# Where two sums are made: VectorE, GpSimd and PSUM in a hybrid of convolution, attention and experts

## The chip, the cores and the metric

The kernel runs on one core of a Trainium2 chip, in fp32 throughout. The metric is the device time of one execution in microseconds; the lower the better. The core has a TensorE (PE in the profile, its weight loads PEld), which multiplies matrices into PSUM; VectorE (DVE), ScalarE (ACT) and GpSimd (POOL), which work on elements; and SyncE (SP), which here issues the DMAs. The engines run beside each other, each through its own queue in program order, and wait for one another by semaphores.

## What is computed

The input x is 8 images of 128 channels and 36 x 36 places. Two layers follow, each with a residual sum. Cut to what matters:

```python
# layer 0: after a group norm, 1x1 and 3x3 convolutions give x, q, k, v;
# attention from 1296 places to 1156 places, then a 1x1 convolution and tanh
attn = softmax(einsum('ancq,bncd->anbqd', q, k), axis=-1)
a_x  = einsum('bncd,anbqd->anbcq', v, attn)[0]
h    = tanh(conv(concat([x, a_x, v_c]), w_h) + b_h)
x    = x0 + conv(h, w_o) + b_o

# layer 1: tokens t [8, 1296, 128]; additive attention, then experts chosen per expert
q = einsum('bld,ed->ble', ln(t), Wq) + bq
k = einsum('bld,ed->ble', ln(t), Wk) + bk
scores = einsum('bijd,d->bij', tanh(q[:, :, None, :] + k[:, None, :, :]), w) + bw
t = t + einsum('bij,bjd->bid', softmax(scores), ln(t))
t = t + experts(ln(t))          # gate, top 8 tokens of each of 64 experts, two layers, scatter
```

The second line of `concat` that comes from the constant image c0 is a vector and enters as a bias. The additive attention is by far the largest part: 8 x 1296 x 1296 x 128 values of tanh.

## The kernel before

tanh(q + k) is not computed element by element. Features of q and of k are made as exponentials of signed sums of channels, so that a product of matrices gives, for each group of channels, a numerator and a denominator, and the score is a sum of their quotients. Such a pair of products is a slot. SLOTS (lines 48 to 53) lists the NP = 12 slots of a unit: four blocks give two slots each with 32 rows a half, and four give one with 64 rows a half; the latter are slots 2, 5, 8 and 11.

A unit is (image b, chunk c, key tile j): 432 queries against 128 keys. There are 8 x 3 x 10 full units of 12 slots, and 24 with the remaining 16 keys (three slots), so 240 x 12 + 72 = 2952 slots. The main loop (from line 934 on) walks through the slots. The order of work is written out by hand: each engine's queue is what this loop emits. For a slot p it emits

- the steps of background lanes that are due (`take_turns`),
- `numerators(p)`: two products on TensorE (L793) into two PSUM buffers of the pool ps_n, which has four buffers and is shared with all background products (`aux`),
- `denominators(p + LAG)`, three slots ahead: two products (L793) into a buffer d, Ln of them on ACT (L815), and after every second slot Exp of the negated Ln (L818), which makes reciprocals lq,
- `terms(p)` on VectorE: numerator times lq,
- a background matmul turn if one is due (`matmul_turn`; PACE and `balance` space them: each turn counts its columns, each slot earns 370).

`terms` has two ways. In most slots VectorE multiplies each half from PSUM into a buffer rp in SBUF (L846; the pool rpp has three buffers) and GpSimd adds both halves to accp in one instruction (L851 for slot 1, L853 later; slot 0 has no add of its own). In the slots of DVE_PAIRS (line 58) VectorE multiplies within PSUM (L836, L840) or into accd (L835) and adds both halves to accd itself (L837, L842). At the end of a unit `sums` puts accp's halves and accd together on GpSimd (L860, L863), and seven slots later ACT makes the exponential e of the scores (L878).

The background lanes hold generators that yield between a turn of matmuls and the step that takes its result out of PSUM. Three matter here. `attend` follows a chunk: for each of its four groups of 108 queries, products of e with the normalized tokens xh (and a column of ones, which gives the denominator) go in two turns into pa; the first is copied to sums in SBUF (L625), the second added to it (L628), then come the reciprocal of the last column (L630), the product with it and the residual token t (L631) and the statistics (L635, L636). `layer0` prepares the next image: for each of three chunks it makes the exponentials e of the scores (L381), their running sum tot on GpSimd (L374), then five turns of products pa with the values, summed in ax (L395, L397), then the column sum pt of tot by a product with ones, its reciprocal ri as Exp of a negated Ln on ACT (L405, L406), and ax times ri (L412), added to the 1x1 convolution px (L413). Query features qf for the coming chunk (L593 on ACT, L594 on GpSimd) come during the chunk's last unit. After the last unit the experts run alone (from line 971 on).

Of the kernel before, what the change touches and what calls it, by code (L numbers as in the profile page):

```python
# [10 lines left out]
AF = mybir.ActivationFunctionType  # L11
ALU = mybir.AluOpType
AX = mybir.AxisListType

NB, C, H, W = 8, 128, 36, 36
N = H * W
HV, WV = H - 2, W - 2
D = HV * WV
CH = 432
NCH = N // CH  # L20
RC = H // NCH
T = 108
# [5 lines left out]
DT = 116  # L28
DTILES = [(o, min(DT, D - o)) for o in range(0, D, DT)]
NDT = len(DTILES)  # L30
# [24 lines left out]
IN_TURN = [m + i for m in range(NF // 2) for i in (0, NF // 2)]  # L55
LAG = 3
SHIFT = 6.5
DVE_PAIRS = (2, 5, 8, 11)
PACE = 370

REM_SLOTS = [([q + m for m in range(NF // 2)], rows) for q, rows in SLOTS[:3]]
# [3 lines left out]
def kernel(  # L65
# [28 lines left out]
    nc = tc.nc  # L94
# [26 lines left out]
    with ExitStack() as loop, ExitStack() as score:  # L121
# [25 lines left out]
        def chunk_tile(name):  # L147
            return chunks.tile([128, CH], F32, tag="chunk", name=name)

        def aux(name):  # L150
            return ps_n.tile([128, 512], F32, tag="n", name=name)
# [25 lines left out]
        ones = const.tile([128, 128], F32, tag="ones", name="ones")  # L177
# [47 lines left out]
        TAKE = (False, 1)  # L225

        def step(rest=1):
            return (False, rest)

        def matmuls(rest=0):  # L230
            return (True, rest)
# [3 lines left out]
        def bmm(out, lhsT, rhs, **kw):  # L235
            behind[0] += max(out.free_size(), 128) + 20
            mm(out, lhsT, rhs, **kw)  # L237
# [91 lines left out]
        def layer0(b):  # L329

            r = xs[b][:, :N]
            k = convolved.pop("k")
            while gates:
                yield step()
            wv_t = load_taps(w_v, "wv_t")
            v = big_tile("v0")
            wq_t = load_taps(w_q, "wq_t")
            yield matmuls(3)
            for r0, nr in KROWS:
                yield from conv_turns(  # L340
                    wv_t, (r0, nr), 1, 1, WV, v[:, r0 * WV : (r0 + nr) * WV]
                )
            yield matmuls(1)

            vw = big_tile("vw")[:DT, : NDT * C].rearrange("p (j c) -> p j c", c=C)
            for g in range(0, NDT, 4):
                some = DTILES[g : g + 4]
                tp = aux("pvw")
                for j, (o, n) in enumerate(some):
                    bmm(tp[:n, j * C : (j + 1) * C], v[:, o : o + n], wh_s[:, 1, :],  # L350
                       start=True, stop=True)
                yield TAKE
                full = sum(n == DT for _, n in some)
                nc.vector.tensor_copy(
                    vw[:, g : g + full, :],
                    tp[:DT, : full * C].rearrange("p (j c) -> p j c", c=C),
                )
                for j in range(full, len(some)):
                    n = some[j][1]
                    nc.vector.tensor_copy(vw[:n, g + j, :], tp[:n, j * C : (j + 1) * C])  # L360
                yield matmuls()
            hp = big_tile("hpre")[:, :N]
            for c in range(NCH):
                cols = slice(c * CH, (c + 1) * CH)
                q = chunk_tile("q0")
                yield from conv_turns(wq_t, (c * RC, RC), 0, 0, W, q)
                yield matmuls(1)
                tot = chunk_tile("tot0")
                ex = []

                def total(j):
                    n = DTILES[j][1]
                    of = ex[0] if j == 1 else tot
                    nc.gpsimd.tensor_add(tot[:n], of[:n], ex[j][:n])  # L374

                for o, n in DTILES:
                    ps = aux("s0")
                    bmm(ps[:n, :CH], k[:, o : o + n], q, start=True, stop=True)
                    yield TAKE
                    e = chunk_tile("e0")  # L380
                    nc.scalar.activation(e[:n], ps[:n, :CH], AF.Exp)  # L381
                    ex.append(e)
                    if len(ex) > 2:
                        total(len(ex) - 2)
                    yield matmuls()
                ax = chunk_tile("ax0")
                for j0 in range(0, NDT, 2):
                    pa = aux("pa0")
                    for j in (j0, j0 + 1):
                        n = DTILES[j][1]  # L390
                        bmm(pa[:, :CH], vw[:n, j, :], ex[j][:n], start=(j == j0), stop=(j > j0))
                    yield TAKE
                    if j0 == 0:
                        total(NDT - 1)
                        nc.vector.tensor_scalar(ax, pa[:, :CH], 1.0 / D, None, ALU.mult)  # L395
                    else:
                        nc.vector.scalar_tensor_tensor(  # L397
                            ax, pa[:, :CH], 1.0 / D, ax, ALU.mult, ALU.add
                        )
                    yield matmuls()  # L400
                pt = aux("pt0")
                bmm(pt[:, :CH], ones[:DT], tot[:DT], start=True, stop=True)
                yield TAKE
                ri = chunk_tile("ri0")
                nc.scalar.activation(ri, pt[:, :CH], AF.Ln, scale=1.0 / D)  # L405
                nc.scalar.activation(ri, ri, AF.Exp, scale=-1.0)  # L406
                yield matmuls(1)
                px = aux("px1")
                bmm(px[:, :CH].rearrange("p (a b) -> p a b", b=W), wh_s[:, 0, :],
                   xpad[:, 1 + c * RC : 1 + (c + 1) * RC, 1 : 1 + W], start=True, stop=True)  # L410
                yield TAKE
                nc.vector.tensor_mul(ax, ax, ri)  # L412
                nc.vector.tensor_add(hp[:, cols], px[:, :CH], ax)  # L413
                yield matmuls()
            yield step(2)
            nc.scalar.activation(hp, hp, AF.Tanh, bias=hb)
            nc.scalar.preload_act_table_set(LNEXP)
            yield matmuls(2)
            for c in range(NCH):
                cols = slice(c * CH, (c + 1) * CH)  # L420
                po = aux("po0")
                bmm(po[:, :CH], wo_s, hp[:, cols], start=True, stop=True)
                yield TAKE
                nc.vector.scalar_tensor_tensor(
                    r[:, cols], po[:, :CH], bo_s, r[:, cols], ALU.add, ALU.add
                )
                yield matmuls()
# [173 lines left out]
        def attend(b, c, es):  # L601


            xh, _, xr = prepared[b]
            if c == 0:
                t2 = big_tile("t2").rearrange("p (t c) -> p t c", c=128)
                mv = two.tile([T, NT, 2], F32, tag="t2_mv", name="t2_mv")
                attended[b] = (t2, mv)
            t2, mv = attended[b]
            for i in range(TPC):  # L610
                at = c * TPC + i
                nc.sync.dma_start(t2[:T, at, :], tokd[b][at * T : (at + 1) * T])
                sums = two.tile([T, C + 1], F32, tag="sums", name="sums")
                for some in (range(6), range(6, NKT)):
                    pa = aux("pa1")[:T, : C + 1]
                    for j in some:
                        if j < NKT - 1:
                            e, v = es[j][:, i * T : (i + 1) * T], xh[:, j, :]
                        else:
                            rows = slice(32 * i, 32 * i + REM)  # L620
                            e, v = es[j][rows, :T], xr[rows]
                        bmm(pa, e, v, start=(j == some[0]), stop=(j == some[-1]))
                    yield TAKE
                    if j < NKT - 1:
                        nc.vector.tensor_copy(sums, pa)  # L625
                        yield matmuls()
                    else:
                        nc.vector.tensor_add(sums, pa, sums)  # L628
                inv = small.tile([T, 1], F32, tag="inv", name="inv")
                nc.vector.reciprocal(inv, sums[:, C : C + 1])  # L630
                nc.vector.scalar_tensor_tensor(  # L631
                    t2[:T, at, :], sums[:, :C], inv, t2[:T, at, :], ALU.mult, ALU.add
                )
                st = small.tile([T, 6], F32, tag="t2_st", name="t2_st")
                nc.vector.bn_stats(st, t2[:T, at, :])  # L635
                nc.vector.bn_aggr(mv[:, at, :], st)  # L636
                yield matmuls()
            if c == NCH - 1:
                prepared.pop(b)
            if b == NB - 1:  # L640
                yield from gate_logits(b, [c])
# [292 lines left out]
        for p, (u, k) in enumerate(slots):  # L934
            b, c, j = units[u]
# [213 lines left out]
```

## Time and profile before

Times are microseconds. Three runs of the kernel before and the profiled execution:

| | us |
|---|---|
| median of 3 runs | 6438.8 |
| lowest, highest | 6434.69, 6439.65 |
| the profiled execution, its own time | 6428.4 |
| its span | 6426.7 |

The profile is one execution, with a mean granted TensorE clock of 0.966. A busy time is the time in which an engine executed something; its share is of the span. A group is all instructions of a line, engine and shape; "idle before" is the time that the engine stood still just ahead of them, with what ended it. Rows of the slots and of the two background parts:

| line, engine, what | count | busy us | mean ns |
|---|---|---|---|
| L846 DVE, product into rp (128 x 432) | 3984 | 2202.6 | 600 |
| L840 DVE, product within PSUM (128 x 432) | 1440 | 811.7 | 608 |
| L842 DVE, sum into accd (128 x 432) | 1440 | 867.4 | 602 |
| L853 POOL, both halves into accp (128 x 864) | 1464 | 2965.2 | 2025 |
| L860, L863 POOL, end of a unit (128 x 432) | 264, 240 | 290.8, 265.6 | 1101, 1107 |
| L815 ACT, Ln of both halves | 2952 | 2552.6 | 882 |
| L818 ACT, Exp over two slots (128 x 1728) | 1464 | 2406.8 | 1644 |
| L628, L630, L631 DVE, attend | 96 each | 28.0, 15.7, 87.9 | 292, 164, 915 |
| L397, L412 DVE, attention of layer 0 | 96, 24 | 58.3, 19.6 | 607, 816 |

Between a short head (about 200 us, before the first slots) and a tail (about 200 us, the experts) the busy shares are even: the slots of one image run beside the preparation of the next and the gating of the last.

### The profile page before, as it was taken

The numbers are of one execution on the slowest core, as the hardware profiler recorded it, in microseconds if no ns is written. First come the engines' busy times: TensorE is split into PE (matmuls) and PEld (weight loads), VectorE is DVE, ScalarE is ACT, GpSimd is POOL, SyncE is SP. The second block draws the span as 40 slices with busy tenths as digits, with TensorE's granted clock in tenths as the row PEclk, the third lists the DMA queues.
The fourth block names the chain that finished last, engine by engine and source line by source line (L and its number), as shares of the span: only waits on it lengthen the run. The fifth ranks groups of instructions, "written<-read, shape, count | busy, mean of one in ns | idle before, by whom it ended". The sixth has DMA issues, their size and how long they took to land.

```text
span 6426.7 us, 106771 instructions
## 1 busy us (share of the span) xinstructions
PE 6054.8 (94%) x40448; PEld 2813.9 (44%) x40448; DVE 4900.4 (76%) x9315; ACT 5354.6 (83%) x5426; POOL 4798.1 (75%) x2966
## 2 busy tenths in 40 slices
PE   8999999999999999999999999999999999999986
PEld 4444444444444444444444444444444444544432
DVE  3687778877788777888788887887778877778862
ACT  1788898888888888888888888888888888989970
POOL 3677777787777877777787787778777787888870
PEclk9999999999999999999999999999999999999997
DMA  0200011000110002100111001100011000100017
GB/s 28 66 31 23 22 63 36 30 24 27 56 46 19 24 27 68 33 26 22 44 47 38 22 23 53 43 32 25 20 63 43 23 24 27 61 26 28 24 66 253
DMA packets 155284, 265.78 MB, mean 41 GB/s; under 512 B 53712, under 2 KB 79824, under 8 KB 154768
## 3 DMA queue, kind: packets, MB, share of 16 engines
q1 hardware_dynamic: 154768, 258.95, 12.5%
q8 instruction: 318, 5.21, 0.3%
q14 instruction: 198, 1.62, 0.1%
HBM read 196.81 MB, written 61.83 MB: 40 GB/s over the span
## 4 chain that ended last, share of the span: by engine, by line
PE 67%; DVE 12%; ACT 7%; issue 7%; POOL 6%; DMA 1%; SPq 0%; POOLq 0%; DVEq 0%; ACTq 0%
PE n L793 30%; PE d L793 10%; PE pc L237 7%; PE pa L237 6%; ACT lq L815 5%; DVE n L840 3%; DVE rp L846 3%; PE s L237 3%; PE pk L237 3%; PE pq L237 2%; DVE accd L842 2%; POOL accp L853 2%; DVE t L631 1%; PE n L800 1%; POOL t L681 1%
## 5 line engine op out<-in xcount | busy, mean ns | idle before, releaser
L853 POOL TENSOR_TENSOR accp<-accp,rp 128x864 f32<-128x864 f32 x1464 | 2965.2, 2025 | 1028.0 <-DVE rp L846 975.3
L793 PE MATMUL n<-qf,kf 32*128 32x432 f32 (+1 forms) x11520 | 3239.2, 579 | 93.4 <-DVE rp L846 47.0
L815 ACT ACTIVATE lq<-d 128x864 f32<-128x864 f32 x2952 | 2552.6, 882 | 690.7 <-PE d L793 643.3
L793 PE MATMUL d<-qf,kf 32*128 32x432 f32 (+1 forms) x11520 | 2876.6, 568 | 21.2 <-ACT lq L815 16.4
L846 DVE TENSOR_TENSOR rp<-n,lq 128x432 f32<-128x432 f32 x3984 | 2202.6, 600 | 623.7 <-PE d L793 399.3
L818 ACT ACTIVATE lq<-lq 128x1728 f32<-128x1728 f32 x1488 | 2429.0, 1632 | 47.1
L793 PEld LDWEIGHTS n<-qf,kf 32*128 32x128 f32 (+1 forms) x11520 | 1167.1, 187 | 1703.4 <-DVE rp L846 586.3
L793 PEld LDWEIGHTS d<-qf,kf 32*128 32x128 f32 (+1 forms) x11520 | 1038.8, 188 | 392.2 <-issue 254.1
L840 DVE TENSOR_TENSOR n<-n,lq 128x432 f32<-128x432 f32 x1440 | 811.7, 608 | 280.1 <-PE n L793 239.2
L842 DVE TENSOR_TENSOR accd<-n,accd 128x432 f32<-128x432 f32 x1440 | 867.4, 602 | 24.7
L851 POOL TENSOR_TENSOR accp<-rp 128x864 f32<-128x864 f32 x264 | 533.8, 2022 | 221.1 <-DVE rp L846 217.5
L237 PE MATMUL pa<-xh,e 128*108 128x129 f32 x1920 | 262.6, 284 | 55.6 <-DVE rp L846 34.7
L860 POOL TENSOR_TENSOR accp<-accp 128x432 f32<-128x432 f32 x264 | 290.8, 1101 | 16.2
L237 PEld LDWEIGHTS pa<-xh,e 128*108 128x108 f32 x1920 | 223.3, 175 | 179.1 <-DVE rp L846 107.4
L594 POOL TENSOR_SCALAR qf<-qf,cs_s 128x432 f32<-128x432 f32 x192 | 262.7, 1374 | 42.0 <-ACT qf L593 42.0
L863 POOL TENSOR_TENSOR accd<-accp,accd 128x432 f32<-128x432 f32 x240 | 265.6, 1107 | 28.5 <-DVE accd L842 10.4
L237 PE MATMUL s<-q,k 128*116 128x432 f32 x480 | 229.8, 570 | 3.3 <-DVE q L260 2.1
L237 PEld LDWEIGHTS pk<-xT,a_k 128*128 128x128 f32 x1408 | 172.2, 193 | 109.8 <-DVE accd L842 27.6
L374 POOL TENSOR_TENSOR tot<-tot,e 116x432 f32<-116x432 f32 x192 | 212.0, 1104 | 6.1
L835 DVE TENSOR_TENSOR accd<-n,lq 128x432 f32<-128x432 f32 x240 | 144.9, 604 | 91.6 <-PE n L793 60.5
L381 ACT ACTIVATE e<-s 116x432 f32<-116x432 f32 x240 | 125.0, 521 | 106.6 <-PE s L237 105.5
L237 PE MATMUL pk<-xT,a_k 128*128 128x128 f32 (+1 forms) x1408 | 203.2, 288 | 2.6 <-DVE accd L842 2.3
(175 smaller groups left out, 4144.4 us busy)
## 6 DMA issues: line engine op xcount, KB each, us to landing
kf<-kd SPq DMA_DIRECT2D x240, 512.0 KB
kd<-ks SPq DMA_DIRECT2D x160, 256.0 KB
w<-in_weight_dram SPq DMA_DIRECT2D x32, 1024.0 KB
x<-in_x_dram SPq DMA_DIRECT2D x8, 648.0 KB
t<-tokd SPq DMA_DIRECT2D x96, 54.0 KB
t2d<-t2T SPq DMA_DIRECT2D x24, 216.0 KB
res<-t2d SPq DMA_DIRECT2D x8, 648.0 KB
out_dram<-res SPq DMA_DIRECT2D x8, 648.0 KB
```

The costliest lines, as they stand in the source:

```text
L237: mm(out, lhsT, rhs, **kw)
L594: nc.gpsimd.tensor_scalar(qf[:, 1, :], qf[:, 0, :], cs_s[:, q : q + 1], None, ALU.mult)
L793: mm(outs[h][:, :CH], kf[rows[h], q, :], qf_of[b, c, q][rows[h], part, :], start=True, stop=True)
L815: nc.scalar.activation(lq[:, o : o + 2, :], d[:, :, :CH], AF.Ln)
L818: nc.scalar.activation(some, some, AF.Exp, scale=-1.0)
L840: mult(ns[h], ns[h], lq[:, o + h, :])
L842: nc.vector.tensor_add(live["d"], ns[h], live["d"])
L846: mult(rp[:, h, :], ns[h], lq[:, o + h, :])
L851: nc.gpsimd.tensor_add(live["p"], live["r"], rp)
L853: nc.gpsimd.tensor_add(live["p"], live["p"], rp)
L860: nc.gpsimd.tensor_add(s[:, 0, :], s[:, 0, :], s[:, 1, :])
L863: nc.gpsimd.tensor_add(d, s[:, 0, :], d)
```

## The change

DVE_PAIRS loses slot 11, so that its products go into rp and its sum to GpSimd, ahead of `sums`. In `attend` the second sum is written over pa in PSUM instead of sums in SBUF, and the reciprocal and the product read it there. In `layer0` the first partial product is copied without the factor 1/D, and Ln of pt loses it too; the middle ones are plain sums; pt with its Ln and Exp comes ahead of the last of the five turns; the last sum is written over pa in PSUM, and the product with ri reads it from there, ahead of the turn of px.

```diff
-DVE_PAIRS = (2, 5, 8, 11)
+DVE_PAIRS = (2, 5, 8)
@@ layer0
                 ax = chunk_tile("ax0")
+                ri = chunk_tile("ri0")
                 for j0 in range(0, NDT, 2):
-                    pa = aux("pa0")
+                    if j0 == NDT - 2:
+                        pt = aux("pt0")
+                        bmm(pt[:, :CH], ones[:DT], tot[:DT], start=True, stop=True)
+                        yield TAKE
+                        nc.scalar.activation(ri, pt[:, :CH], AF.Ln)
+                        nc.scalar.activation(ri, ri, AF.Exp, scale=-1.0)
+                        yield matmuls()
+                    pa = aux("pa0")[:, :CH]
                     for j in (j0, j0 + 1):
                         n = DTILES[j][1]
-                        bmm(pa[:, :CH], vw[:n, j, :], ex[j][:n], start=(j == j0), stop=(j > j0))
+                        bmm(pa, vw[:n, j, :], ex[j][:n], start=(j == j0), stop=(j > j0))
                     yield TAKE
                     if j0 == 0:
                         total(NDT - 1)
-                        nc.vector.tensor_scalar(ax, pa[:, :CH], 1.0 / D, None, ALU.mult)
+                        nc.vector.tensor_copy(ax, pa)
+                    elif j0 < NDT - 2:
+                        nc.vector.tensor_add(ax, pa, ax)
                     else:
-                        nc.vector.scalar_tensor_tensor(
-                            ax, pa[:, :CH], 1.0 / D, ax, ALU.mult, ALU.add
-                        )
+                        nc.vector.tensor_add(pa, pa, ax)
+                        nc.vector.tensor_mul(ax, pa, ri)
                     yield matmuls()
-                pt = aux("pt0")
-                bmm(pt[:, :CH], ones[:DT], tot[:DT], start=True, stop=True)
-                yield TAKE
-                ri = chunk_tile("ri0")
-                nc.scalar.activation(ri, pt[:, :CH], AF.Ln, scale=1.0 / D)
-                nc.scalar.activation(ri, ri, AF.Exp, scale=-1.0)
-                yield matmuls(1)
                 px = aux("px1")
...
                 yield TAKE
-                nc.vector.tensor_mul(ax, ax, ri)
                 nc.vector.tensor_add(hp[:, cols], px[:, :CH], ax)
@@ attend
                     if j < NKT - 1:
                         nc.vector.tensor_copy(sums, pa)
                         yield matmuls()
-                    else:
-                        nc.vector.tensor_add(sums, pa, sums)
+                nc.vector.tensor_add(pa, pa, sums)
                 inv = small.tile([T, 1], F32, tag="inv", name="inv")
-                nc.vector.reciprocal(inv, sums[:, C : C + 1])
+                nc.vector.reciprocal(inv, pa[:, C : C + 1])
                 nc.vector.scalar_tensor_tensor(
-                    t2[:T, at, :], sums[:, :C], inv, t2[:T, at, :], ALU.mult, ALU.add
+                    t2[:T, at, :], pa[:, :C], inv, t2[:T, at, :], ALU.mult, ALU.add
                 )
```

## The prediction

> **What bounds the kernel now.** I read the page first (shares of the engines, the chain), then the chain summed by line, then the waits, then single lines and one stretch of the timeline, last a table of stretches for the engine that gets the work. The page:
>
> ```profile
> span 6426.7 us, 106771 instructions
> PE 6054.8 (94%) x40448; PEld 2813.9 (44%) x40448; DVE 4900.4 (76%) x9315; ACT 5354.6 (83%) x5426; POOL 4798.1 (75%) x2966
> PE 67%; DVE 12%; ACT 7%; issue 7%; POOL 6%; DMA 1%; SPq 0%; POOLq 0%; DVEq 0%; ACTq 0%
> ```
>
> Four engines are busy between 75% and 94%, and no single one is full: the chain that ended last is two thirds TensorE, 12% VectorE and 6% GpSimd. The DVE part is where the change can save, the POOL part where it can lose. The chain by line shows which DVE instructions those are:
>
> ```profile
> by line: PE n L793 30.4%; PE d L793 9.6%; PE pc L237 7.2%; issue 6.9%; PE pa L237 6.4%; ACT lq L815 4.9%; DVE n L840 3.3%; DVE rp L846 3.0%; PE s L237 3.0%; PE pk L237 2.7%; PE pq L237 2.1%; DVE accd L842 1.7%; POOL accp L853 1.6%; DVE t L6
> ```
>
> L840 and L842 are the products and sums of slots 5, 8 and 11, whose sums VectorE makes. They have 5.0% of the chain with 3 x 240 slots; L846, the products of all other slots, has 3.0% with 1992 (3984 instructions, two a slot). The reason is in the waits (who waited for whom, us in total, times, longest):
>
> ```profile
> PEld n L793 <- DVE accd L842: 248.3, 535, 3.3
> DVE rp L846 <- POOL accp L851: 78.1, 32, 8.7
> DVE rp L846 <- POOL accp L853: 3.1, 5, 1.1
> ```
>
> The numerators of a later slot need the PSUM buffers of an earlier one, and where VectorE sums, it holds them for four instructions instead of two. The other two lines are the reverse: VectorE wants an rp buffer that GpSimd has not added up yet. That is rare today, 37 times and 81 us of 6427.
>
> One more DVE line stands out, the product of attend (durations min/median/max), and the timeline beside it says why:
>
> ```profile
> L631 DVE SCALAR_TENSOR_TENSOR t<-sums,inv,t x96: 350/674/1841, 456.6 to 6274.5; 108x128 f32<-108x128 f32 x96
> ...
> 3018.48 2.02 POOL L853 TENSOR_TENSOR accp<-accp,rp 128x864 f32<-128x864 f32 x1 [0.75 <-DVE rp L846]
> ...
> 3019.03 1.61 DVE L631 SCALAR_TENSOR_TENSOR t<-sums,inv,t 108x128 f32<-108x128 f32 x1
> ```
>
> A 0.35 us instruction took 1.61: it began 0.55 us into a GpSimd add and ended at 3020.64, just after that add's end at 3020.50.
>
> **What the Trainium skill says.** "SBUF — State Buffer", section "Who interferes with whom": a VectorE instruction with two SBUF inputs contends with a GpSimd instruction that reads SBUF, and the one that comes second blocks until the first is done; with at most one SBUF input, outside the two-port modes, it does not. The trace agrees twice: L631 reads sums and t, both in SBUF, and spreads from 350 to 1841 ns; L846 reads PSUM and SBUF and stays within 542 to 611 ns over 3984 instructions beside a GpSimd that is 75% busy. "PSUM — Partial Sum Buffer", section "Specifications (TRN2)": VectorE reads and writes PSUM, at most one tensor input from there. The new forms keep to that, and writing into PSUM costs nothing here: L840 (PSUM to PSUM) has a mean of 608 ns, L846 (PSUM to SBUF) 600. The engine prices come from rows: 602 ns for an L842 add, 2025 ns for an L853 add over both halves.
>
> **The change part by part.** The sum is made against the profiled execution's own 6428.4 us (span 6426.7, 1.7 around it); the median of the runs is 10.4 higher, and I add that at the end.
>
> A. Slot 11 leaves VectorE: 240 x 2 L842 adds go, 289 us of DVE work (480 x 0.602). Its products become L846 products and its PSUM buffers come free after two instructions. What that is on the path, from the chain: 5.0% of 6426.7 is 321 us for three slot kinds, so 107 for slot 11; as an ordinary slot it still has L846's share, 193 us / 1992 x 240 = 23. Saved: 84 us. Bounds: nothing, if TensorE's own queue or ACT (83% busy) is late next everywhere; 289 us if every add stood on the path, which a 12% DVE share excludes as a likely value. I take 84.
>
> B. The same slot reaches POOL: 240 more L853 adds of 2.025 us, 486 us, so POOL goes from 75% to 82% of an unchanged span. Its idle time today is 1629 us, so on average the work fits. It does not everywhere. Five of the ten full units of one chunk, us of the stretch and then the busy us (and instructions) of PE, PEld, DVE, ACT and POOL, the granted clock and the DMA columns:
>
> ```profile
> 1280.30:1303.90 23.60, 23.39 (x117) 9.58 (x116) 19.28 (x36) 21.04 (x22) 16.82 (x11) 1.00 0.08 22
> 1303.90:1331.40 27.50, 27.11 (x356) 11.87 (x358) 18.57 (x33) 24.19 (x28) 26.46 (x19) 1.00 0.08 23
> ...
> 1384.90:1410.40 25.50, 25.11 (x122) 9.83 (x126) 18.43 (x34) 23.35 (x28) 24.91 (x18) 1.00 0.07 25
> 1410.40:1432.80 22.40, 22.02 (x113) 8.91 (x106) 18.75 (x34) 21.05 (x22) 16.77 (x10) 1.00 0.08 21
> 1432.80:1458.50 25.70, 24.76 (x113) 9.64 (x116) 19.58 (x35) 23.67 (x28) 23.78 (x16) 1.00 0.05 12
> ```
>
> A plain unit has some 6 us to spare; the three of the ten that also carry the attention's running total (L374) or the query products (L594) have 1.0, 0.6 and 1.9 and get 2.0 more: 2.5 us over per chunk, 60 us over 24 chunks if nothing took it up. Much is taken up by the plain unit behind it; what isn't appears as VectorE waiting for an rp buffer. In the queue, slot 11's add stands just ahead of the two adds of sums (1.1 us each), which stand ahead of L851 of the next unit; so L851, the one waited for today, ends up to 2.0 us later. The 37 waits of today grow by 2.0 (75 us), and I estimate that as many more that just miss today grow by half of that (37): 112 us of DVE idle. VectorE's waits reach the end only where TensorE has no other work, so half: +55. Bounds 0 and +146 (three loaded units a chunk, 2.025 us each, 24 chunks). What else waits behind POOL is TensorE's transposes of t and xh (L681, L538); this is inside the bound.
>
> C. Attend. L628's sum goes to PSUM, still one instruction (294 ns, taken unchanged), the reciprocal reads one PSUM column (164), and the product now has one SBUF tensor: 915 mean becomes about 350, its minimum, 96 times: 54 us. L631 takes 1.5% to 1.7% of the chain in the stretches of 1000 us from 1200, 2200 and 4200 us, 15 to 17 us, and is busy about as much there (96 x 0.915 = 88 us over six such stretches), so nearly all of it is on the path; TensorE's next numerators are late next, so I take 80%: -43. Against it, the pa buffer is held through reciprocal and product, about 0.6 us longer; in a pool of four the numerators two slots on can want it. Nobody waits for L628 in the trace. Bounds 0 and 96 x 0.6 = 58, taken +10. In the queue behind the product stand the two statistics and the terms of the slot, which move up.
>
> D. Attention of layer 0: the final product changes from ax, ri (two SBUF inputs, 816 mean, 1329 at most) to pa, ri; 24 x 0.21 = 5 us saved. The ax chain has seven DVE instructions before and after at about 607 each; 1/D goes from both sides and removes no instruction. The sum of the exponentials (pt) comes one turn earlier and its Ln and Exp (512 and 563 ns) have one turn less before the DVE add and product need ri. ACT's queue ahead of them holds at most a pair's Exp, so a stall of 0.2 to 0.5 us behind which the slot's terms queue: 24 x 0.2 = 5. Net 0, bounds -5 and +25. The running total has still three turns of pa before pt, so POOL is not late for it.
>
> Sum: -84 + 55 - 43 + 10 = -62; 6428.4 - 62 = 6366, and with the 10.4 the predicted median is 6377 us, 1.0% faster.
>
> **The rivals.** R1, slower: POOL becomes the bound at the ends of loaded units. A lag above some 4.5 us (three slots of about 2.17 us between a product and the reuse of its rp buffer, less the add's 2.0) stops VectorE, and with it the release of PSUM and TensorE. For it: three units in ten go over their length, and the L851 waits already reach 8.7 us. Against it: the six spare microseconds of the plain units. Price: +146 from B, +10 from C, A down to 60 because those units don't gain, C's 43: +53, or about 6492. R2, VectorE was the tighter bound: half of the 289 us is gained (-145), the plain units take up most of POOL's work (+15), C gives its whole 54 and no buffer is late: -184, 6255. For it: the DVE is 68% to 84% busy in the stretches above and stands between TensorE's numerators and their buffers; against it, ACT's 83%. R3, A and B cancel: what VectorE doesn't wait for in PSUM it waits for in rp. Then C alone stays, -33, 6406.
>
> **How the numbers follow.** Forecast 0.37 (its own range 6340 to 6395), R2 and what lies between 0.16, R3 0.22, R1 0.25. A measurement here tells 0.2% (13 us) from no change. Faster by more: the forecast, R2 and half or more of R3, 0.64; within: the upper end of R3 and the lower of R1, 0.10; slower 0.26. The range 6270 to 6485 leaves out the extremes of R2 and R1.
>
> **What would show it.** A right: L842 has 960 instructions, and the waits of PEld n for accd fall by a third or more from 248 us. B right: L853 x1704, POOL at 82 to 84%, and the waits of DVE rp for POOL between 130 and 250 us; over 350 is R1. C right: L631's median near 350 with a maximum under 450; wrong if it still spreads. D right: no DVE wait for ri above 10 us. The whole is wrong if POOL's share of the chain rises by more than DVE's falls.

## The result, and the profile after

The changed kernel takes 6512.6 us (median of 4 runs, 6503.9 to 6528.4) where the kernel before takes 6436.7: a ratio of 1.0123, with a 95% interval from 1.0100 to 1.0145. It is 1.2% slower, 79 us by the ratio (76 between the two medians); the forecast was 1% faster, and the time lies above the range that it gave.

The page of the changed kernel: span, busy shares, chain by engine.

```profile
span 6526.6 us, 107021 instructions
PE 6181.5 (95%) x40448; PEld 2868.2 (44%) x40448; DVE 4595.9 (70%) x8835; ACT 5368.6 (82%) x5426; POOL 5270.3 (81%) x3206
PE 66%; POOL 11%; DVE 8%; issue 7%; ACT 6%; DMA 1%; SPq 0%; POOLq 0%; ACTq 0%; DVEq 0%
```

VectorE lost 304 us of busy time (4900 to 4596) and GpSimd gained 472, about as counted. The chain shows what that did: DVE went from 12% to 8%, POOL from 6% to 11%. The forecast had named a POOL share that rises by more than DVE's falls as the sign that it would be wrong as a whole.

The waits of the changed kernel (who waited for whom, us in total, times, longest):

```profile
PEld n L793 <- DVE accd L842: 204.3, 393, 3.4
DVE rp L846 <- POOL accp L851: 163.5, 91, 5.5
DVE rp L846 <- POOL accp L853: 112.8, 79, 4.0
```

VectorE's waits for an rp buffer rose from 81 us (37 times) to 276 (170 times). The waits on accd fell only from 248 to 204.

The product of attend is now L631 with pa as its input (durations min/median/max), and here the forecast, a median near 350 ns and a maximum under 450, holds:

```profile
L631 DVE SCALAR_TENSOR_TENSOR t<-pa,inv,t x96: 349/351/353, 461.7 to 6372.6; 108x128 f32<-108x128 f32 x96
```

Where is the time? The unit of image 4, chunk 2, key tile 6 is the costliest place. In the windows view (stretch, its length, busy us of PE, PEld, DVE, ACT and POOL, granted clock, DMA columns) it took this before:

```profile
3918.30:3943.90 25.60, 22.29 (x121) 10.75 (x119) 18.82 (x36) 20.29 (x20) 25.20 (x23) 0.85 0.07 25
```

and this after:

```profile
3970.90:4004.10 33.20, 26.65 (x136) 12.37 (x135) 18.00 (x33) 22.93 (x23) 27.93 (x20) 0.90 0.12 36
```

Its timeline after, GpSimd and VectorE alone:

```profile
3975.11 2.01 POOL L853 TENSOR_TENSOR accp<-accp,rp 128x864 f32<-128x864 f32 x1
3977.11 1.56 POOL L539 TENSOR_SCALAR xh<-tok,ln_mv,ln_rs 128x128 f32<-128x128 f32 x2
3978.65 2.01 POOL L853 TENSOR_TENSOR accp<-accp,rp 128x864 f32<-128x864 f32 x1
3980.73 1.10 POOL L860 TENSOR_TENSOR accp<-accp 128x432 f32<-128x432 f32 x1
3981.91 1.10 POOL L863 TENSOR_TENSOR accd<-accp,accd 128x432 f32<-128x432 f32 x1
3983.00 2.33 POOL L539 TENSOR_SCALAR xh<-tok,ln_mv,ln_rs 128x128 f32<-128x128 f32 x3
3985.31 1.99 POOL L851 TENSOR_TENSOR accp<-rp 128x864 f32<-128x864 f32 x1
...
3980.69 1.12 DVE L846 TENSOR_TENSOR rp<-n,lq 128x432 f32<-128x432 f32 x2 [0.73 <-POOL accp L853]
3981.73 0.68 DVE L557 COPY xT<-tpc 128x512 f32<-128x512 f32 x1
3987.33 1.12 DVE L846 TENSOR_TENSOR rp<-n,lq 128x432 f32<-128x432 f32 x2 [4.92 <-POOL accp L851]
```

From 3975.11 on GpSimd has no gap of 0.1 us for over 12 us: adds of the slots, the normalized tokens xh of the next image, the end of the unit (L860, L863), and only then the add of slots 0 and 1 (L851) that sets an rp buffer free. VectorE stands still for 4.92 us until 3987.33, and numerators and Ln wait behind it too. In the images 1 to 6 the unit of chunk 2, key tile 6 is 5 to 11 us longer than before.

### The profile page after: what moved, and what is told of

It reads as the page before. It is cut to its first block, busy times and chain, and to the rows that moved or that the text cites. A ratio compares the mean times of both kernels' runs of the same rounds, so it can differ in the third digit from the quotient of the medians.

```text
span 6526.6 us, 107021 instructions
## 1 busy us (share of the span) xinstructions
PE 6181.5 (95%) x40448; PEld 2868.2 (44%) x40448; DVE 4595.9 (70%) x8835; ACT 5368.6 (82%) x5426; POOL 5270.3 (81%) x3206
## 4 chain that ended last, share of the span: by engine, by line
PE 66%; POOL 11%; DVE 8%; issue 7%; ACT 6%; DMA 1%; SPq 0%; POOLq 0%; ACTq 0%; DVEq 0%
PE n L793 29%; PE d L793 10%; PE pc L237 7%; PE pa L237 7%; POOL accp L853 5%; ACT lq L815 4%; DVE rp L846 3%; PE s L237 3%; PE pk L237 2%; DVE n L840 2%; POOL accp L851 2%; PE pq L237 2%; PE d L800 1%; DVE accd L842 1%; POOL qf L595 1%
## 5 line engine op out<-in xcount | busy, mean ns | idle before, releaser
L853 POOL TENSOR_TENSOR accp<-accp,rp 128x864 f32<-128x864 f32 x1704 | 3447.7, 2023 | 889.7 <-DVE rp L846 823.4
L793 PE MATMUL n<-qf,kf 32*128 32x432 f32 (+1 forms) x11520 | 3332.3, 586 | 122.6 <-DVE rp L846 83.9
L846 DVE TENSOR_TENSOR rp<-n,lq 128x432 f32<-128x432 f32 x4464 | 2464.4, 600 | 1112.0 <-PE d L793 488.2
L793 PE MATMUL d<-qf,kf 32*128 32x432 f32 (+1 forms) x11520 | 2997.3, 573 | 46.1 <-ACT lq L815 42.3
L793 PEld LDWEIGHTS n<-qf,kf 32*128 32x128 f32 (+1 forms) x11520 | 1203.2, 189 | 1788.5 <-DVE rp L846 712.5
L793 PEld LDWEIGHTS d<-qf,kf 32*128 32x128 f32 (+1 forms) x11520 | 1078.4, 190 | 428.0 <-issue 245.2
L840 DVE TENSOR_TENSOR n<-n,lq 128x432 f32<-128x432 f32 x960 | 543.9, 609 | 191.3 <-PE n L793 136.2
L842 DVE TENSOR_TENSOR accd<-n,accd 128x432 f32<-128x432 f32 x960 | 577.8, 602 | 16.4
L851 POOL TENSOR_TENSOR accp<-rp 128x864 f32<-128x864 f32 x264 | 533.9, 2022 | 14.4 <-DVE rp L846 14.3
L860 POOL TENSOR_TENSOR accp<-accp 128x432 f32<-128x432 f32 x264 | 291.1, 1102 | 20.4
L237 PE MATMUL pa<-xh,e 128*108 128x129 f32 x1920 | 268.3, 287 | 37.2 <-DVE t L631 16.5
L863 POOL TENSOR_TENSOR accd<-accp,accd 128x432 f32<-128x432 f32 x240 | 265.1, 1105 | 18.8
L237 PE MATMUL pa<-e,vw 116*128 116x432 f32 x480 | 203.1, 549 | 1.6 <-DVE rp L846 0.6
```

The costliest lines, as they stand in the source:

```text
L793: mm(outs[h][:, :CH], kf[rows[h], q, :], qf_of[b, c, q][rows[h], part, :], start=True, stop=True)
L840: mult(ns[h], ns[h], lq[:, o + h, :])
L842: nc.vector.tensor_add(live["d"], ns[h], live["d"])
L846: mult(rp[:, h, :], ns[h], lq[:, o + h, :])
L851: nc.gpsimd.tensor_add(live["p"], live["r"], rp)
L853: nc.gpsimd.tensor_add(live["p"], live["p"], rp)
```

## The experiments

All ratios are of a run against the kernel before on the same chip, with 95% intervals. Unless a diff says otherwise it is against the kernel before.

**psum_only**: the changed kernel with DVE_PAIRS = (2, 5, 8, 11), so parts C and D alone.

> The kernel before with the PSUM edits of attend and layer0 alone; slot 11's sum stays on VectorE. Theory 1 (the loss is GpSimd's added work at places where it is loaded, and the PSUM part is harmless or good): 6385 to 6437 us, L631 at about 350 ns; within this, the predicted saving of part C would be 6400 or less, and 6425 to 6437 would mean that the shorter product is hidden. Theory 3 (the pa buffers held longer in PSUM, or pt one turn earlier, cost the time): 6490 us or more.

1.0027 (1.0018 to 1.0036). This fits neither theory: 6446 us, no gain where 33 us were forecast, and no loss of the size of theory 3. Two opposite effects were possible, so it was split later.

**pairs_only**:

```diff
-DVE_PAIRS = (2, 5, 8, 11)
+DVE_PAIRS = (2, 5, 8)
```

> The kernel before with slot 11's sum on GpSimd alone. Theory 1: 6510 to 6560 us, the whole loss and no less, with DVE rp waiting for POOL over 250 us in total. Theory 3: 6380 to 6440 us.

1.0078 (1.0066 to 1.0090), 6477 us. Moving slot 11's sum is a loss, but not the whole one, so theory 1 was too simple. VectorE waited 271 us for GpSimd here (184.6 for L851, 86.7 for L853), about as in the changed kernel.

**sum_left_out**, against the changed kernel:

```diff
-                else:
+                elif k < 11:
                     nc.gpsimd.tensor_add(live["p"], live["p"], rp)
```

> The changed kernel without GpSimd's add of slot 11: the products are made, their sum is left out of the score. VectorE has the relief of part A, GpSimd has no more work than before. If part A is worth its 84 us and C its 33: about 6320 us. If VectorE's relief is hidden by the other engines: 6395 to 6437 us. Theory 3: over 6480 us.

0.9951 (0.9938 to 0.9965). Against psum_only the relief of VectorE is worth 0.76%, 49 us: neither 84 nor nothing. Against the changed kernel, GpSimd's 240 adds cost 1.72%, 111 us.

**added_load**:

```diff
                     for h in range(2):
                         nc.vector.tensor_add(live["d"], ns[h], live["d"])
+                    if k == 11:
+                        nc.gpsimd.tensor_add(live["l"], live["l"], live["l"])
...
                 rp = rpp.tile([128, 2, CH], F32, tag="rp", name="rp")
...
+                live["l"] = rp
```

> The kernel before plus one GpSimd add of 128 x 864 in each full unit just after VectorE's slot 11, over the rp buffer of slot 10, which nobody reads any more; nothing else changes. Theory 1: the added 486 us of GpSimd work alone cost 60 to 150 us, 6500 to 6590 us. If GpSimd's slack takes it up: 6437 us within 15, and the loss would have to come from slot 11's own rp buffer or from VectorE's new order.

1.0096 (1.0082 to 1.0110). GpSimd work that nobody needs, on an engine that idles 25% of the span, costs 0.96%. So the load costs time without slot 11's move; the added instruction also keeps slot 10's rp buffer until it is done, so load and buffer are not told apart here.

**attend_only**: the edit of `attend` and nothing else.

> The kernel before with attend's sum and product in PSUM and nothing else. Theory P (the PSUM part's loss of 0.27% comes from layer0's new order, and attend gains where it runs): 0.990 to 0.997 of before, with the units of key tiles 1 and 2, where attend runs, about 1 us shorter each. Theory H (pa held longer is what costs): 1.002 to 1.006.

0.9930 (0.9918 to 0.9943). This is theory P, and 45 us: most of the 54 us taken from L631 count. Compared slot by slot, the gain lies in the units of key tiles 1 and 2 (1.1, 2.0 and 1.2 us a unit of tile 1 in the three chunks), and nearly all others are unchanged.

**layer0_only**: the edit of `layer0` and nothing else.

> The kernel before with layer0's edit (pt one turn earlier, the last sum and product in PSUM) and nothing else. Theory P: 1.004 to 1.010, with the time lost in the units of chunk 2, key tiles 4 to 6, where the token work of GpSimd falls. Theory H: 0.998 to 1.002.

1.0094 (1.0080 to 1.0108). So the edit that the forecast priced at nothing costs 60 us. On average over the images, the units of chunk 2, key tiles 4 and 6, are 3.5 and 5.3 us longer; the short unit between them is 2.5 us shorter. Another place is far from the tokens: the unit of chunk 0, key tile 3 is 1.9 us longer. In it TensorE waits for wxn, scaled weights of the next image's group norm that GpSimd makes (L302), before and then in layer0_only:

```profile
PE pb L237 <- POOL wxn L302: 6.6, 2, 4.9
PE pb L237 <- POOL wxn L302: 30.0, 7, 4.9
```

**rest_only**:

```diff
                 nc.scalar.activation(ri, ri, AF.Exp, scale=-1.0)
-                yield matmuls(1)
+                yield matmuls()
```

> The kernel before with one token changed: after Ln and Exp of the attention's sum, layer0 rests for no slot instead of one, as in the changed kernel. All that follows in the background lane (tokens among it) moves up by up to three slots an image. If the shift alone causes layer0's loss: the same as layer0_only within 0.3%, 1.004 to 1.010. If the loss is in the new order itself (ri late, PSUM held): 0.998 to 1.002.

1.0146 (1.0129 to 1.0163). One slot of rest taken out, no instruction changed, and 94 us are lost, more than from the whole edit. In GpSimd's queue the xh instructions now begin behind slot 7's add of the unit of key tile 5, before behind slot 10's; in ACT's queue the tanh of layer 0 moves from slot 9 of key tile 4 to slot 6. But the run changes one thing more. Without the rest, the product with ri follows the Exp sooner, and VectorE waits for it: 3.8 us in the kernel before, and here

```profile
DVE ax L412 <- ACT ri L406: 26.1, 21, 1.5
```

So this run is not the place alone.

**layer0_rest_kept**, against layer0_only: `yield matmuls(1)` after the Exp of ri.

> layer0_only with the one slot of rest after Ln and Exp put back, so that the tokens' work on GpSimd falls where it fell in the kernel before. If only the shift cost the 0.94% of layer0_only: 0.997 to 1.002. If the new order costs in itself (ri late for VectorE, pa held in PSUM): 1.004 to 1.010 again.

1.0108 (1.0094 to 1.0122). It did not test what it was meant to: the trace has the xh instructions in the same slots as layer0_only. The background lane earns 370 columns a slot and a turn of pa costs 904, so a slot of rest ahead of pa is made up for by the budget.

**psum_rest_kept**, against psum_only, and **after_rest_kept**, against the changed kernel, with the same line:

> Both PSUM edits with slot 11's sum on VectorE and the slot of rest put back: the candidate for the fastest. If the shift is all that is bad in them: 0.990 to 0.994, at or a little below attend_only (0.993). If layer0's edit is bad in itself: above 0.997.

> The changed kernel with the slot of rest put back. The terms measured one by one, attend -0.7%, slot 11 +0.8%, layer0 without its shift about 0, give 1.000; up to 1.006 if slot 11's add costs more beside the other edits, as in the changed kernel against the run without the sum (1.7% between them). Still 1.010 or more would mean that the shift has no part in the changed kernel's loss.

1.0028 (1.0021 to 1.0035) and 1.0115 (1.0099 to 1.0132): as without it. Both failed for the same reason and tell nothing of the place.

**layer0_placed**, against layer0_only:

```diff
                         nc.vector.tensor_mul(ax, pa, ri)
-                    yield matmuls()
+                    yield matmuls(2 if j0 == NDT - 2 else 0)
```

> layer0_only with two slots of rest ahead of the turn of px, which puts the tokens' work on GpSimd back to the place in the order that it has in the kernel before (for all images but the first that is prepared this way); the order of pt and pa, and the last sum and product in PSUM, stay as changed. If layer0's loss is the place of the tokens' work: 0.998 to 1.003. If it is the edit itself: 1.007 to 1.011 again.

0.9990 (0.9982 to 0.9998). The same instructions with the tokens' work, and all that follows in the lane, in its old place: the loss of 0.94% is gone. GpSimd's timeline around the end of the unit of image 4, chunk 2, key tile 5 shows the two places. Before:

```profile
3918.63 2.02 POOL L853 TENSOR_TENSOR accp<-accp,rp 128x864 f32<-128x864 f32 x1
3920.64 1.57 POOL L538 TENSOR_SCALAR xh<-tok,ln_mv,ln_rs 128x128 f32<-128x128 f32 x2
3922.19 1.08 POOL L860 TENSOR_TENSOR accp<-accp 128x432 f32<-128x432 f32 x1
3923.35 1.11 POOL L863 TENSOR_TENSOR accd<-accp,accd 128x432 f32<-128x432 f32 x1
3924.44 3.12 POOL L538 TENSOR_SCALAR xh<-tok,ln_mv,ln_rs 128x128 f32<-128x128 f32 x4
3927.53 2.01 POOL L851 TENSOR_TENSOR accp<-rp 128x864 f32<-128x864 f32 x1
```

and layer0_only, whose lines stand one or two lower (L852 is the add of slots 0 and 1, L847 the product into rp), GpSimd and then VectorE:

```profile
3947.00 3.13 POOL L539 TENSOR_SCALAR xh<-tok,ln_mv,ln_rs 128x128 f32<-128x128 f32 x4
3950.09 2.02 POOL L854 TENSOR_TENSOR accp<-accp,rp 128x864 f32<-128x864 f32 x1
3952.09 1.57 POOL L539 TENSOR_SCALAR xh<-tok,ln_mv,ln_rs 128x128 f32<-128x128 f32 x2
...
3955.63 1.56 POOL L539 TENSOR_SCALAR xh<-tok,ln_mv,ln_rs 128x128 f32<-128x128 f32 x2
3957.17 1.09 POOL L861 TENSOR_TENSOR accp<-accp 128x432 f32<-128x432 f32 x1
3958.34 1.11 POOL L864 TENSOR_TENSOR accd<-accp,accd 128x432 f32<-128x432 f32 x1
3959.43 2.33 POOL L539 TENSOR_SCALAR xh<-tok,ln_mv,ln_rs 128x128 f32<-128x128 f32 x3
3961.74 1.99 POOL L852 TENSOR_TENSOR accp<-rp 128x864 f32<-128x864 f32 x1
...
3963.77 1.12 DVE L847 TENSOR_TENSOR rp<-n,lq 128x432 f32<-128x432 f32 x2 [6.37 <-POOL accp L852]
```

Before, two of the eleven xh instructions stand ahead of the unit's end (L860), four between it and L851, and five come later. Shifted, eight stand ahead, three between, none later. All of the burst is queued ahead of the add that frees the rp buffer, and VectorE waits 6.37 us at once. In sum, though, VectorE's waits for GpSimd's adds are 113 us in layer0_only and 81 in the kernel before, so these waits themselves make at most about half of the 60 us.

**where_attend**, against attend_only:

```diff
+        def light(u):
+            return units[u][2] in (1, 2)
...
-            if k in DVE_PAIRS and not rem:
+            if k in DVE_PAIRS and not rem and (k < 11 or not light(u)):
```

> attend_only, and slot 11's sum on GpSimd only in the units of key tiles 1 and 2, in which attend loads VectorE and GpSimd has room; elsewhere VectorE keeps it. If VectorE's relief pays there and only there: another 0.002 to 0.006 below attend_only, the fastest of all. If it does not pay anywhere: equal to attend_only within 0.1%. If GpSimd's load costs everywhere: above attend_only.

0.9978 (0.9968 to 0.9988), above attend_only. Against it, the units of tiles 1 and 2 are unchanged within 0.3 us; the unit after them in the first chunk, where the gating of the last image has its GpSimd work (L681), is 2.8 us longer. I read this as the add's lag, carried into the next unit.

**rp_four**, against the changed kernel, with room made:

```diff
-        kstp = pool("kstp", 3, score, "right")
+        kstp = pool("kstp", 2, score, "right")
...
-        rpp = pool("rpp", 3, score, "right")
+        rpp = pool("rpp", 4, score, "right")
...
-            st = small.tile([128, NKT, 6], F32, tag="ln_st", name="ln_st")
+            st = const.tile([128, NKT, 6], F32, tag="ln_st", name="ln_st")
```

> The changed kernel with four rp buffers instead of three (room made by two instead of three ks buffers and a single ln_st). If what costs is that VectorE has to wait for the third rp buffer in GpSimd's bursts, a fourth takes 2 us of lag more each time: 1.002 to 1.007 instead of 1.0123. If GpSimd's rate or the half clock after a stall sets it, little changes: 1.009 to 1.013.

0.9928 (0.9915 to 0.9940): better than the best that was expected. GpSimd is as loaded as in the changed kernel (5272 us); the waits of VectorE for it, in rp_four:

```profile
DVE rp L846 <- POOL accp L853: 49.9, 44, 3.0
DVE rp L846 <- POOL accp L851: 24.3, 12, 2.8
```

They fell from 276 to 74 us. A fourth buffer takes up most of the waits that GpSimd's bursts made. That this is no gain of the change, and that GpSimd's load still costs with four, the next runs show.

**before_four**, **attend_four** and **pairs_attend_four**: the kernel before, attend_only, and attend_only with DVE_PAIRS = (2, 5, 8), each with the four buffers.

> The kernel before with four rp buffers (and two ks buffers and one ln_st, which make room). If three buffers hold the kernel only once slot 11's add is on GpSimd: 0.996 to 1.001. If they held it already: 0.985 to 0.993, and the changed kernel's 0.9928 with four would be no gain of the change at all.

> attend_only with four rp buffers. If the two gains are of different waits and add up: attend_only's 0.993 times before_four's ratio, within 0.002.

> attend_four with slot 11's sum on GpSimd as well. If VectorE's relief is worth its 84 us once GpSimd's lag has room: 0.005 to 0.012 below attend_four. If the relief is hidden by ACT and TensorE, as the plain units' unchanged times in the runs so far suggest: within 0.003 of attend_four.

0.9920 (0.9906 to 0.9933), 0.9839 (0.9826 to 0.9852), 0.9848 (0.9835 to 0.9861). The kernel before gains the fourth buffer's 0.8% as well, so rp_four's gain is no gain of the change: with four buffers in both, the changed kernel and the kernel before are equal within noise (0.9928 and 0.9920). Attend's gain and the buffer's add up (0.9930 x 0.9920 = 0.9851). Moving slot 11's sum changes nothing that is clear of noise. pairs_attend_four and rp_four differ by layer0's edit alone: with four buffers it still costs 0.80%. attend_four, 6326 us, is the fastest kernel here that computes everything. The two smaller edits that make room were not run alone.

**left_out_four**, against pairs_attend_four, with the edit of sum_left_out, and **added_load_four**, against attend_four, with the edit of added_load:

> pairs_attend_four without GpSimd's add of slot 11: the products are made, their sum is left out of the score. VectorE has the relief, GpSimd no added work. If the relief is hidden by ACT and TensorE: 0.982 to 0.985, as attend_four. If it is worth what the run without the sum showed with three buffers (0.76% against psum_only): 0.975 to 0.978, and slot 11's move is then a gain and a cost of one size.

> attend_four plus one GpSimd add of 128 x 864 in each full unit after VectorE's slot 11, over slot 10's rp buffer, which nobody reads any more. With three buffers this load alone cost 0.96%. If four buffers take it up: 0.984 to 0.987. If the load costs by itself: 0.990 or more.

0.9766 (0.9752 to 0.9781) and 0.9906 (0.9889 to 0.9922). The four corners: relief without load -0.73%, load without relief +0.67%, both +0.09%. The relief is real, and GpSimd's add costs as much as it saves, with four buffers. With three, the same add cost 1.72% (sum_left_out to the changed kernel) and the added load 0.96%.

## Why the prediction was wrong

The runs make a path from the kernel before to the changed one, one part at a step, so its steps add up to the whole (1% is 64 us):

| part | forecast us | step of the path | measured |
|---|---|---|---|
| C, attend | -43 + 10 | before to attend_only, 1 to 0.9930 | -0.70%, -45 us |
| D, layer 0 | 0 (-5 to +25) | to psum_only, 1.0027 | +0.97%, +62 us |
| A, relief of VectorE | -84 | to sum_left_out, 0.9951 | -0.76%, -49 us |
| B, load on GpSimd | +55 (0 to +146) | to the changed kernel, 1.0123 | +1.72%, +111 us |
| sum | -62 | | +1.23%, +79 us |

The forecast misses by 141 us: 62 from D, 56 from B, 35 from A, and C took 12 off.

**D is the step that failed.** It was priced as seven VectorE instructions against seven and one turn less for ri, and its bounds held only what stands in those lines. What it did not count is the rest: `yield matmuls(1)` became `yield matmuls()`, and a generator that is earlier in its last turns starts all that follows it in the lane earlier. Here that is the tanh, the eleven xh instructions of 0.79 us and the rsqrt before them, some three slots earlier. The new order of turns moves it too: with pt ahead of the last pa, the same rest put back behind pt does not bring the old place back (layer0_rest_kept). The stall that the forecast feared, of VectorE on ri, is not in the changed kernel: no wait of VectorE for ri is among those listed. layer0_placed shows that the place is the cause: the full edit with the lane in its old place costs nothing (-0.10%). rest_only agrees, with VectorE's wait for ri mixed in.

How the place costs time is shown only in part. The xh burst ahead of the add that frees an rp buffer is one way, TensorE's longer waits for wxn another. The rp buffers can't be all of it: with four of them D is still +0.80%. The rest stays open; the last section has a candidate.

**B was mis-sized by half.** The picture of L851, late behind slot 11's add and the sums of the unit, is in the trace; waits for L853, only 3 us before, grew as well, to 113. The size of the waits was nearly right: 112 us more of VectorE's idle were forecast, and in B's own step (sum_left_out to the changed kernel) the two lines of waits went from 149 to 276 us, 127 more. What failed is "half reaches the end": the step cost 111 us. From the changed kernel to rp_four the waits fell by 202 us and the time by 1.95%, 125 us. Nor do these waits explain all of the price: with four buffers the same step (left_out_four to pairs_attend_four) costs 0.82%, 53 us, while they grow by 14 us only (43 to 57). D's shift is not shown to matter for B: pairs_only, without C and D, has A and B at +0.78% together, the path has +0.96%, within noise of it. The 276 us of waits lie between the band given for the forecast (130 to 250) and R1's (over 350); GpSimd came to 81% of the span, a little under the 82 to 84% named.

**A was mis-sized the other way.** The chain's share of L840 and L842 gave 84 us, the runs 49 (47 with four buffers), somewhat over half. A likely reason, which no run isolates, is that the chain counts a VectorE step as if nothing else were nearly late. The waits on accd, which were to fall by a third, fell by 18%; in A's own step, psum_only to sum_left_out, they fell by a third (292 to 196 us), since D's edit had raised them first (to 291 in layer0_only).

**C was right**, and the time gained even more than the forecast: the product, which took up to 1.8 us beside a GpSimd add, takes 349 to 353 ns, as "SBUF — State Buffer", section "Who interferes with whom", says of an instruction with one SBUF input, and 45 us came where 33 were forecast. The waits for which 10 us were taken off, of numerators for the pa buffer, did come. In attend_only, whose lines stand one higher, numerators wait for the product (L630):

```profile
PEld n L792 <- DVE t L630: 8.2, 24, 0.4
```

In the changed kernel it is 14.2 us, 45 times; before, nobody waited for L628, which then set pa free. (One more wait, of 16.5 us in the changed kernel, stands at the end of the last chunk, behind a transfer of t that came late before too.) The sum of the new L628 into PSUM takes 297 ns, into SBUF it took 292.

The rival R1 had the mechanism, GpSimd's lag in loaded units, and with 6492 us nearly the size, but it kept D at nothing and came to its time by a B of 146, larger than the 111 measured: the near hit is luck. R2's relief of 145 us is out. R3's cancelling of A and B is what four buffers give, not three.

## What to carry to other kernels

Where background work is paced by yields, an edit that drops a rest or reorders turns moves everything behind it: list which bursts on a busy engine move, and what stands in their queue there, before you price the edit at nothing. When you put a rest back, look in the trace whether the old place is back too. An engine with a quarter of its span idle can still cost time when it gets more work: 240 adds on GpSimd cost 111 us with three buffers between it and VectorE and 53 with four; try one more buffer before moving work off or onto it. A VectorE instruction with two tensors in SBUF beside a busy GpSimd is worth a PSUM operand, if the data is there anyway.

## What the runs showed that was not expected

A part of the lost time may be paid in TensorE's clock. The changed kernel's mean granted clock is 0.951, the kernel before has 0.966, attend_four 0.971 and left_out_four 0.973. In the traces each record of it is 1 or 0.5. Between the first slots and the experts (from 250 us after the start to 230 us before the end) it is 0.5 for 294 us before and for 481 us in the changed kernel. These stretches follow stalls: before, TensorE was idle for 56% of the 3.4 us ahead of a fall to 0.5, on average over the 41 falls, and for 4% of the time of the slots as a whole. At half clock a matmul of L793 over 432 columns has a median of 924 ns, at full clock 522.

TensorE is busy for 265 us of the half clock before and for 448 in the changed kernel. An estimate from these figures: 183 x (1 - 522/924) = 80 us more of TensorE time, against 100 us between the two profiled executions, if everything waited for TensorE in those stretches; it is rough, as matmuls overlap. The profile pages point the same way: with the same 40448 matmuls TensorE's busy time grew by 127 us, and its idle time fell from 372 to 345. So a stall may be paid twice, once as a wait and again as slower matmuls after it, and the second may be the larger part. No run isolates this, since the clock can't be held while the waits change, and it is not so at every place: the unit of key tile 6 shown above had 0.85 before and 0.90 after.

It is also open why the relief is worth only 49 us of the 289 us that leave VectorE; no run loaded or relieved ACT, which is the fullest engine after TensorE.
